# Layer 0 of a four-layer gated Flamingo stack: the first two expert routings ahead of other side jobs, two guessed experts' weights loaded before the first plan

## Chip, cores and metric

The kernel runs on one core of one Trainium2 chip. The metric is the device time of one execution in microseconds (us); lower is better. All data are float32 unless said otherwise.

## What is computed

The input x has 16 sequences of 128 tokens with 256 features; ctx has the same shape. Four layers follow each other, each a gated attention and a gated feed-forward part:

```
for i in 0..3:
    x = x + tanh(g_xattn[i]) * attention_i(layernorm(x), ctx)
    x = x + tanh(g_ffn[i])   * ffn_i(layernorm(x))
```

Attentions 0 to 2 have 16 heads of 16 features (attention 1 takes its softmax over the queries, attention 2 has a key mask), attention 3 has 8 heads of 64. The feed-forward parts of layers 0, 2 and 3 are mixtures of 8 experts with the top 2 per token; that of layer 1 is a dense layer with a routed low-rank addition. Layer 0's mixture, the one that matters here:

```
gate = softmax(x @ w_gate.T)                      # 8 experts
topk_scores, topk_idx = top_k(gate, 2)
h = gelu(x @ W1[e] + b1[e]); y = h @ W2[e] + b2[e]   # 256 -> 1024 -> 256
out = sum over the two chosen experts of score * y
```

## The kernel before, in words

**Tiles.** x stays in SBUF as 16 tiles of 128 tokens. Work goes in four blocks of four tiles. An attention is a loop over 16 items (one tile each): `scores(n)`, `values(n-1)`, `output(n-2)`, in `attend` (from L1411). `output` adds the result to x and `ready` takes the tile's layer-norm statistics (`mean_var`, L248, bn_stats and bn_aggr).

**Side jobs.** Everything else in the attention phase is a Python generator, a *job*, cut into stages by `yield`. `yield 1` asks for the next stage on DVE, `yield Act(1)` on ACT, `yield Pe(1)` on PE. For every block there are jobs that prepare the next block (layer norm, queries, keys; `prepare`, L1160), and when a block's last output is out, a *behind* job: in layers 0, 2 and 3 the routing `Moe.front` (L457). At the start of each block of items the loop waits until the preparing jobs are done.

**The planner.** While the kernel is being built, `Clock` (L1342) keeps a modelled time for PE, ACT, DVE and POOL, and `attend` places a job's next stage when the model says that its inputs are there and its engine's queue is short (`poll`, `whole`, `idle`, `Tick`). PE, ACT and DVE then execute in exactly this order. The orders of SP's and POOL's queues are chosen by the framework from modelled readiness, not by hand. Times of the model are not times of the chip.

**Routing and plan.** `Moe.front` normalises a block, computes router logits, picks the top two (`first_max` twice), gets each row's place by a rank matmul and running offsets, and POOL scatters each tile's rows twice into a DRAM table `xg` (8 indirect DMAs per block, L552). `xg` was filled with zeros before (`clear`, 15 DMAs of 1170 KB). After block 1 and after block 3 of layer 0 a *plan* (`Moe.plan`, L621) turns the counts into slots: a slot is 128 rows of one expert. The first plan holds only full slots, and 9 of them are certain for two blocks, whatever the routing; the second plan holds the other 30. A plan gives each slot its expert (row 0), its place (row 1) and *new* (row 2): 0 if the lane's weights are already those of this expert.

**Slots and lanes.** `Moe.slots` (L721) runs the slots of a plan. A lane is a set of weight buffers (w1 and w2 of 1024 KB, b1 4 KB, b2 128 KB). The first nine slots go over two lanes alternately: lane 0 takes the first five slots of the plan, lane 1 the last four, so the second slot executed is the sixth of the plan. Per slot SP reads plan values, loads the rows (`load`: xr, L782), and issues `first` (w1, b1, b2) and `second` (w2); a load whose *new* is 0 is skipped on the chip (`fetch`, L1575). PE transposes the rows (L815), computes the hidden layer (L1624), ACT takes Gelu (L1629), PE the second product (L852), DVE scales (L860), POOL scatters the result (L864). The slots are `attend`'s *filler*: its PE stages are placed only once all 16 items have had their scores; the PE stages of other jobs go ahead of it.

**Layer 1.** Its softmax sums run over the queries, per key. `Fast16.scores` sums four exponential tiles of 128x512 (L1264 to L1276): for two of them POOL first adds the two halves into a 128x256 tile (L1269), for the others DVE reduces all 512 columns (L1273).

Of the kernel before, what the change touches and what calls it, by code (L numbers as in the profile page):

```python
# [90 lines left out]
def kernel(ctx: ExitStack, tc: tile.TileContext, a: dict, out: bass.AP):  # L91
# [156 lines left out]
    def mean_var(mv, i, src):  # L248
        st = stat.tile([P, 6], F32, tag="bnst", name="bnst", bufs=4)
        nc.vector.bn_stats(st, src)  # L250
        nc.vector.bn_aggr(mv[:, i, :], st)

# [188 lines left out]
    class Moe:  # L441
# [4 lines left out]
        def __init__(self, layer, wg, turn, see=None):  # L446
            self.layer, self.wg, self.turn, self.see = layer, wg, turn, see
            self.off = rpool.tile([P, B + 1, NE], F32, tag="off", name="off", bufs=1)
            nc.gpsimd.tensor_copy(self.off[:, 0], region)
            self.carry = region  # L450
            self.done = None
            self.passed = 0
            self.scatters, self.returns, self.weighted = [], [], []

# [3 lines left out]
        def front(self, blk, plan=None, bias=None):  # L458


            own_set = run["fast"] and blk == NBLK - 1
            xns, xnT = yield from ln_block(blk, self.see, own_set, True)
            if bias is not None:
# [4 lines left out]
            next(soft)  # L468
            yield Act(1)
            next(soft)  # L470
# [10 lines left out]
            hot = self.kept([P, 2, BPB, NE], "hot")  # L481
            yield 1
            first_max(hot[:, 0], key, m, xns[:, :, D + 3])
            yield 1
            key2 = small("key2")
# [44 lines left out]
            )  # L530
            yield 3
            while self.passed < blk:
# [88 lines left out]
        def plan(self, turns, early=False, kind=""):  # L621
# [70 lines left out]
            nexts = [0] + ends[:-1]  # L692
            for lane in nexts:
                nc.vector.memset(plan[:, 2, lane:lane + 1], 1.0)

# [24 lines left out]
        def slots(self, n, plans, lanes, get, fetch1, fetch2, hidden, nf, far, depth):  # L720
# [151 lines left out]
            for s in range(near):  # L872
                load(s)
                first(s)
                if s < near2:
                    second(s)
# [6 lines left out]
            for s in range(n):  # L883
                while not planned(s + far + 1):
                    yield Pe(1)
                first(s + near)
                hT = yield from hidden(get, lane(s), xTs.pop(s), lambda *ps: when(s, *ps))
                if s == 0:
                    turn(1)
                turn(s + 2)  # L890
                hidden_of.append((s, hT))
                if len(hidden_of) > depth:
                    finish(*hidden_of.pop(0))
                weigh(s + 1)
                load(s + far)
                second(s + near2)
                yield Pe(0)
# [230 lines left out]
    class Fast16:  # L1128
# [86 lines left out]
        def scores(self, b, tick):  # L1215
# [45 lines left out]
            if layer == 1:  # L1261
# [4 lines left out]
                for j, e in enumerate(es):  # L1266
                    if j < 2:
                        half = pool.tile([P, 4, S // 2], F32, tag="half", name="half")
                        nc.gpsimd.tensor_tensor(  # L1269
                            half, e[:, :, 0:S // 2], e[:, :, S // 2:], ALU.add  # L1270
                        )
                        e = half
                    nc.vector.tensor_reduce(  # L1273
                        by_pair[:, j], e.rearrange("p (c e) s -> p c e s", e=2), AX.X, ALU.add
                    )
# [66 lines left out]
    class Clock:  # L1342


        def __init__(self):
            self.at = {e: 0.0 for e in (*IN_ORDER, mybir.EngineType.Pool)}
            self.done, self.read, self.rings = {}, {}, {}
            self.mode = None
            self.ends, self.moved = [], []

# [36 lines left out]
        def note(self, ins):  # L1387
# [5 lines left out]
            if "DMA" in type(ins).__name__ or ins.engine not in self.at:  # L1393
                end = max(start, self.at[PE]) + 3.0
                self.moved.append(end)
            else:
                start = max(start, self.at[ins.engine])
                end = start + self.cost(ins, outs[0], srcs)
                self.at[ins.engine] = end
                end += 0.2 if ins.engine == PE else 0.1  # L1400
                self.ends.append(end)
            for x in outs:
                self.done[x.tensor.name] = end
            for x in srcs:
                name = x.tensor.name
# [4 lines left out]

    def attend(parts, filler=None, open_end=False, hurry=True, share=2.5, eager=False):  # L1411

# [5 lines left out]

        clock = Clock()
        n = 0  # L1420
# [24 lines left out]
        def poll():  # L1445
            for job in jobs + filling:
                if job[2] is Pe:
                    continue
# [30 lines left out]
        class Tick:  # L1479
            left = 0.0  # L1480

            def __call__(self, full=True):
                if not full:
                    poll()
                    return
                end = now() + self.left
# [4 lines left out]

            def urgent(self):
                for job in jobs:
                    if job[3] and job[2] is Pe and max(job[1], bank()) <= now() + 0.1:
                        run_stage(job)
                        self.urgent()
                        return
# [24 lines left out]
        with tc.manual_schedule(engines=IN_ORDER):  # L1522
# [5 lines left out]
            for n in range(len(steps) + 2):  # L1528
# [22 lines left out]
                if n >= 2:  # L1551
                    att, b = steps[n - 2]
                    att.output(b, tick)
                    if b % BPB == BPB - 1:
                        _, _, behind, blk = blocks[(n - 2) // BPB]
                        job = begin(behind(blk), int, hurry)
                        waiting.append(job)
                        if len(waiting) <= 2:
                            jobs.append(job)
                    tick()  # L1560
# [6 lines left out]
    def gate_weights(name):  # L1567
# [5 lines left out]
        return wg  # L1573

    def fetch(out, weights, layout, e, new):  # L1575

        nc.sync.dma_start(
            out=out, in_=weights[bass.ds(e, 1)].rearrange(layout, p=P),
            cond=new, bounds_check="skip_entire_dma",
        )  # L1580

    def fetch_columns(out, name, e, new):
        n = out.shape[-1]
        nc.sync.dma_start(
            out=out, in_=a["cols"][:, bass.ds(e * n + _COLS[name][0], n)],
            cond=new, bounds_check="skip_entire_dma",
        )

    def fetch_row(out, rows, e, new):

        nc.sync.dma_start(
            out=out, in_=rows[bass.ds(e, 1), :].to_broadcast([P, D]),
            cond=new, bounds_check="skip_entire_dma",
        )

    def lane0(pool, n):
# [6 lines left out]
        } for _ in range(n)]  # L1603

    def slots0(moe, n, plans, lanes, get):
        nf = F0 // P

        def fetch1(w, e, new):
            fetch(w["w1"], a["l0_w1"], "e (k p) f -> p (e k) f", e, new)
            fetch_columns(w["b1"], "l0_b1", e, new)  # L1610
            fetch_row(w["b2"], a["l0_b2"], e, new)

        def fetch2(w, e, new):
            fetch(w["w2"], a["l0_w2"], "e (c p) d -> p (e c) d", e, new)

# [678 lines left out]
    def layers(fast):  # L2294
# [40 lines left out]
        with tc.tile_pool(name="context", bufs=1) as cpool, ExitStack() as for_mid:  # L2335
# [16 lines left out]
            with tc.tile_pool(name="att0", bufs=2) as pool:  # L2352
# [16 lines left out]
                def clear(blk):  # L2369
                    if blk == 1:  # L2370
# [9 lines left out]
                        for i in range(0, ROWS, n * P):  # L2380
# [268 lines left out]
```

## Time and profile before

| | |
|---|---|
| time, median of 3 runs | 1668.66 us (1667.05 to 1671.42) |
| profiled execution: its own time | 1609.76 us |
| profiled execution: span, first to last instruction | 1607.8 us |
| mean granted TensorE clock | 0.970 |
| busy share: PE, PE weight load, DVE, ACT, POOL | 93%, 73%, 54%, 40%, 24% |
| instructions | 34920 |
| DMA, mean over the span | 105 GB/s |
| layer 0's attention, first scores to last value matmuls | about 25 to 121.7 us |
| layer 0's first nine slots, hidden layers | 145.2 to about 220 us |

A line of the order of instructions reads: start (us from the span's start), duration, engine, source line, operation, output<-inputs, shape, count merged, and in brackets how long the engine was idle before it and what ended that. PE is TensorE's matmuls, PEld its weight loads, DVE VectorE, ACT ScalarE, POOL GpSimd, SPq the queue of SyncE, from which most DMAs are issued; an issue's duration is that of the issue, not of the transfer. A group's line ends in busy us and mean ns of one instruction, then the idle time ahead of them and what ended it.

### The profile page before, as it was taken

The page shows a single profiled execution, that of the slowest core. Times are in us where ns is not written, and L with a number is a line of the kernel's source. Part 1 is how long each engine was busy: PE and PEld are TensorE (multiplying, and loading weights), DVE is VectorE, ACT ScalarE, POOL GpSimd, SP SyncE. Part 2 cuts the span into 40 slices and gives each one's busy share as a digit, 9 for nine tenths or more (in the row PEclk, how much of TensorE's full clock was granted, in tenths as well). Part 3 has the DMA queues.
Part 4 walks back from the last instruction along what each step waited for, and adds up shares of the span by engine and source line. Part 5 has one row for each costly group of instructions (what it writes and reads, how often), then busy time and mean ns, then how long its engine had stood idle before and what let it go on. Part 6 is the DMA issues. An engine that isn't in the chain of part 4 may idle for free.

```text
span 1607.8 us, 34920 instructions
## 1 busy us (share of the span) xinstructions
PE 1493.5 (93%) x12752; PEld 1176.1 (73%) x12752; DVE 860.7 (54%) x2763; ACT 646.7 (40%) x1546; POOL 392.1 (24%) x517
## 2 busy tenths in 40 slices
PE   6994999999988999999999999999999999997992
PEld 4674889999655566665459999999965656677892
DVE  3785412223258776676345555555754437477664
ACT  5663333335546455553224333333453233224110
POOL 4234301112454322434000110111142002023531
PEclk9997999999999999999999999999999999999996
DMA  9606573534420000111064331611242000033956
GB/s 330 256 29 230 175 258 113 185 105 134 96 43 1 1 1 15 55 41 54 0 211 151 100 111 49 211 31 29 88 111 41 1 14 28 1 101 108 315 175 212
DMA packets 107768, 169.29 MB, mean 105 GB/s; under 512 B 17081, under 2 KB 77950, under 8 KB 107584
## 3 DMA queue, kind: packets, MB, share of 16 engines
q1 hardware_dynamic: 83744, 111.99, 22.1%
q0 software_dynamic: 20304, 49.66, 9.9%
q10 hardware_dynamic: 3536, 5.25, 1.0%
q8 instruction: 108, 1.77, 0.5%
q14 instruction: 76, 0.62, 0.1%
HBM read 268.42 MB, written 48.18 MB: 197 GB/s over the span
## 4 chain that ended last, share of the span: by engine, by line


## 5 line engine op out<-in xcount | busy, mean ns | idle before, releaser
L1801 PEld LDWEIGHTS ps_w<-xT,w 128*128 128x128 f32 x2304 | 264.3, 192 | 2.7 <-issue 0.4
L1801 PE MATMUL ps_w<-xT,w 128*128 128x128 f32 x2304 | 265.0, 275 | 0.2 <-issue 0.2
L864 POOL DMA_INDIRECT yd<-y,to x117 | 118.7, 1014 | 565.8 <-DVE c L827 296.8
L852 PE MATMUL ps_e<-w,hT 128*128 128x256 f32 x848 | 198.0, 380 | 2.5 <-DVE hT L1708 1.9
L852 PEld LDWEIGHTS ps_e<-w,hT 128*128 128x128 f32 x848 | 154.5, 190 | 21.6 <-DVE hT L1708 2.8
L1809 ACT ACTIVATE u<-ps_w,b 128x128 f32<-128x128 f32 x312 | 89.7, 368 | 175.8 <-PE ps_w L1801 170.7
L1624 PE MATMUL ps_h<-xT,w 128*128 128x128 f32 x1120 | 137.7, 283 | 12.4 <-DMA w<-in_l_w_dram 11.7
L1624 PEld LDWEIGHTS ps_h<-xT,w 128*128 128x128 f32 x1120 | 136.1, 200 | 15.6 <-issue 14.3
L1812 DVE SCALAR_TENSOR_TENSOR m<-ps_w,b,u 128x128 f32<-128x128 f32 x312 | 87.5, 344 | 109.1 <-PE ps_w L1801 93.8
L1629 ACT ACTIVATE hT<-ps_h,b 128x128 f32<-128x128 f32 x312 | 89.3, 373 | 119.4 <-issue 83.2
L552 POOL DMA_INDIRECT xg<-xn,xi x96 | 93.9, 978 | 108.3 <-issue 60.4
L1738 PE MATMUL ps_w<-xnT,sw 128*128 128x512 f32 x256 | 111.9, 593 | 0.0
L860 DVE SCALAR_TENSOR_TENSOR y<-ps_e,c,bias 128x256 f32<-128x256 f32 x78 | 37.6, 482 | 133.5 <-PE ps_e L852 129.7
L1110 POOL TENSOR_TENSOR sum_range<-sum_range,rs 128x256 f32<-128x256 f32 x48 | 35.4, 737 | 262.2 <-DVE rs L2218 136.3
L1738 PEld LDWEIGHTS ps_w<-xnT,sw 128*128 128x128 f32 x256 | 48.2, 190 | 56.8 <-issue 50.7
L817 DVE COPY xT<-ps_xr 128x256 f32<-128x256 f32 x117 | 48.4, 416 | 73.4 <-PE ps_xr L815 73.4
L1316 DVE RECIPROCAL rs<-ps_o 128x256 f32<-128x256 f32 x32 | 56.1, 1754 | 38.1 <-PE ps_o L1305 30.9
L1258 ACT ACTIVATE e<-ps_s 128x512 f32<-128x512 f32 x128 | 66.0, 602 | 21.8 <-PE ps_s L1243 21.8
L321 ACT ACTIVATE xn<-x,nmr,rstd 128x256 f32<-128x256 f32 x128 | 67.5, 595 | 16.3 <-DVE nmr L314 16.3
L844 ACT ACTIVATE bias<-b,c 128x256 f32<-128x256 f32 x78 | 40.3, 516 | 72.0 <-DMA b<-in_l_b_dram 28.1
L1305 PE MATMUL ps_o<-e,v 128*32 128x128 f32 x1536 | 54.3, 284 | 11.7 <-POOL sum_range L1110 4.7
L2197 ACT ACTIVATE e<-ps_s 128x512 f32<-128x512 f32 x64 | 33.4, 600 | 74.2 <-PE ps_s L2191 74.2
(273 smaller groups left out, 2578.7 us busy)
## 6 DMA issues: line engine op xcount, KB each, us to landing
w<-in_l_w_dram SPq DMA_DIRECT2D x156, 1024.0 KB
w<-in_l_w_dram SPq DMA_DIRECT2D x39, 512.0 KB
kT<-in_l_wgu_dram SPq DMA_DIRECT2D x39, 512.0 KB
xg<-zeros POOLq DMA_DIRECT2D x15, 1170.0 KB, 21.4
xr<-xg SPq DMA_DIRECT2D x78, 130.0 KB
b<-in_l_b_dram SPq DMA_DIRECT2D x78, 128.0 KB
kT<-in_l_w_dram SPq DMA_DIRECT2D x39, 256.0 KB
x<-yd POOLq DMA_DIRECT2D x48, 128.0 KB, 4.9
```

What stands on the lines that cost most here:

```text
L321: nc.scalar.activation(xns[:, i, 0:D], src, AF.Identity, bias=nmr[:, i:i + 1], scale=rstd[:, i:i + 1])
L552: self.unordered(nc.gpsimd.indirect_dma_start(out=xg[:, :], in_=xns[:, i, :], in_offset=None, out_offset=bass.IndirectOffsetOnAxis(ap=xi[: ...
L852: nc.tensor.matmul(po, lhsT=hT[:, f, :], rhs=lane(s)["w2"][:, f, :], start=(f == 0), stop=(f == nf - 1),)
L864: self.unordered(nc.gpsimd.indirect_dma_start(out=yd[:, :], in_=y, in_offset=None, out_offset=bass.IndirectOffsetOnAxis(ap=to[:, 0:1], axi ...
L1258: nc.scalar.activation(e, pss[j], AF.Exp)
L1316: nc.vector.reciprocal(rs, po[:, 1])
L1624: nc.tensor.matmul(ps[:, i, :], lhsT=w["w1"][:, k, f * P:(f + 1) * P], rhs=xT[:, k, :], start=(k == 0), stop=(k == KC - 1),)
L1629: nc.scalar.activation(hT[:, f, :], ps[:, i, :], AF.Gelu, bias=w["b1"][:, f:f + 1])
L1738: nc.tensor.matmul(ps, lhsT=wt[:, k, f * P:(f + 1) * P], rhs=xnT[:, k, :], start=(k == 0), stop=(k == KC - 1),)
L1801: nc.tensor.matmul(ps[:, f, :], lhsT=wt[:, k, s, f * P:(f + 1) * P], rhs=xT[:, k, :], start=(k == 0), stop=(k == KC - 1),)
L1809: nc.scalar.activation(u[:, f, :], pair[0][:, f, :], AF.Identity, bias=w["b1"][:, i:i + 1])
L1812: nc.vector.scalar_tensor_tensor(m1[:, f, :], pair[1][:, f, :], w["b3"][:, i:i + 1], u[:, f, :], ALU.add, ALU.mult,)
```

## The change

1. *Express routing.* In layer 0 the routings of blocks 0 and 1 are *express* (`express=2`): they are put at the head of the job list with priority 2, some of their yields fall away, their DVE and ACT stages are placed as long as the modelled queue is under 4 us, and their PE stages also at the short ticks inside an item.
2. *Guessed weights.* When block 2's preparation starts, all eight loads of lane 0 for expert 0 and of lane 1 for expert 3 are issued without condition, behind the last bn_aggr emitted by then. In the first plan, *new* for the first slot of each lane becomes "expert is not the guessed one" instead of 1. Within a slot b1 and b2 are now loaded ahead of w1. With two lanes, slot 0's w2 is asked for after slot 1's w1.
3. *Planner.* With `eager` (layer 0 only) the model gives DMAs of SP a shared transfer rate and POOL's DMAs an issue time; everywhere DMAs count as starting no earlier than the last plan.
4. *Layer 1.* The halving on POOL is gone; DVE reduces all four tiles over 512 columns.

```diff
-        nc.vector.bn_aggr(mv[:, i, :], st)
+        run["aggr"] = nc.vector.bn_aggr(mv[:, i, :], st).ins
...
+            express = run["fast"] and self.layer == 0 and blk < NBLK // 2
...
             next(soft)
-            yield Act(1)
+            if not express:
+                yield Act(1)
             next(soft)
...
-            yield 1
+            if not express:
+                yield 1
             first_max(hot[:, 0], key, m, xns[:, :, D + 3])
-            yield 1
+            if not express:
+                yield 1
...
-            yield 3
+            if not express:
+                yield 3
             while self.passed < blk:
...
-            for lane in nexts:
-                nc.vector.memset(plan[:, 2, lane:lane + 1], 1.0)
+            for lane, at0 in enumerate(nexts):
+                new = plan[:, 2, at0:at0 + 1]
+                if lane in self.guess:
+                    nc.vector.tensor_scalar(
+                        new, plan[:, 0, at0:at0 + 1], float(self.guess[lane]), None,
+                        ALU.not_equal,
+                    )
+                else:
+                    nc.vector.memset(new, 1.0)
...
-                if s < near2:
+                if s < near2 and near > 1:
                     second(s)
...
                 first(s + near)
+                if s == 0 and near == 1:
+                    second(0)
...
                 for j, e in enumerate(es):
-                    if j < 2:
-                        half = pool.tile([P, 4, S // 2], F32, tag="half", name="half")
-                        nc.gpsimd.tensor_tensor(
-                            half, e[:, :, 0:S // 2], e[:, :, S // 2:], ALU.add
-                        )
-                        e = half
                     nc.vector.tensor_reduce(
...
             if "DMA" in type(ins).__name__ or ins.engine not in self.at:
-                end = max(start, self.at[PE]) + 3.0
+                start = max(start, self.at[PE], self.plan)
+                if not self.loads:
+                    end = start + 3.0
+                elif ins.engine == mybir.EngineType.Pool:
+                    self.at[ins.engine] = max(start, self.at[ins.engine]) + 1.27
+                    end = self.at[ins.engine] + 2.5
+                else:
+                    size = self.free(outs[0]) * list(outs[0].ap)[0][1] * 4
+                    if outs[0].tensor.name in self.done and size > 2e5:
+                        size *= 0.3
+                    self.dma = max(self.dma, start) + size / 250e3
+                    end = self.dma + 2.0
...
             for job in jobs + filling:
-                if job[2] is Pe:
+                while job[3] == 2 and job in jobs and job[2] is not Pe:
+                    queue = max(now(), clock.at[DVE if job[2] is int else ACT])
+                    if job[1] > queue + 0.3 or queue > now() + 4.0 and job[1] > now():
+                        break
+                    run_stage(job)
+                if job[2] is Pe or job[3] == 2:
                     continue
...
                 if not full:
                     poll()
+                    self.urgent(2)
                     return
...
-                        job = begin(behind(blk), int, hurry)
+                        job = begin(behind(blk), int, 2 if blk < express else hurry)
                         waiting.append(job)
                         if len(waiting) <= 2:
-                            jobs.append(job)
+                            jobs.insert(0 if blk < express else len(jobs), job)
...
+    def first0(w, e, new):
+        fetch_columns(w["b1"], "l0_b1", e, new)
+        fetch_row(w["b2"], a["l0_b2"], e, new)
+        return fetch(w["w1"], a["l0_w1"], "e (k p) f -> p (e k) f", e, new)
...
+                    if blk == 2 and fast:
+                        moe.guess = {0: 0, 1: 3}
+                        for get_some in first0, second0:
+                            for lane, e in moe.guess.items():
+                                tc.add_manual_dep(
+                                    get_some(lanes[lane], e, None).ins, run["aggr"].name,
+                                    mybir.DependencyInfo(
+                                        mybir.DependencyClass.Sync,
+                                        mybir.DependencyReason.DATA,
+                                    ),
+                                    reason="behind the first loads",
+                                )
...
-                    attend([(att, clear, behind)], early(), eager=True)
+                    attend([(att, clear, behind)], early(), eager=True, express=2)
```

More of the change, by code (lines that the diff above doesn't have):

```diff
@@ L452, in __init__ @@
             self.passed = 0
+            self.guess = {}
             self.scatters, self.returns, self.weighted = [], [], []
@@ L692, in plan @@
             nexts = [0] + ends[:-1]
-            for lane in nexts:
-                nc.vector.memset(plan[:, 2, lane:lane + 1], 1.0)
+            for lane, at0 in enumerate(nexts):
[7 more added lines that the diff above has]
+                    nc.vector.memset(new, 1.0)
+            self.guess = {}
             nc.vector.tensor_copy(plan[:, 3], end[:, NE - 1:NE].to_broadcast([P, n]))
@@ L1342, with __init__ @@
     class Clock:
-        def __init__(self):
+        def __init__(self, loads):
+            self.loads = loads
             self.at = {e: 0.0 for e in (*IN_ORDER, mybir.EngineType.Pool)}
@@ L1348, in __init__ @@
             self.mode = None
+            self.dma = self.plan = 0.0
             self.ends, self.moved = [], []
@@ L1403, in note @@
                 self.done[x.tensor.name] = end
+                if x.tensor.name.startswith("plan_i"):
+                    self.plan = end
             for x in srcs:
@@ L1409, in when, with attend @@
             return max((self.done.get(t.tensor.name, 0.0) for t in tiles), default=0.0)
-    def attend(parts, filler=None, open_end=False, hurry=True, share=2.5, eager=False):
-        clock = Clock()
+    def attend(parts, filler=None, open_end=False, hurry=True, share=2.5, eager=False, express=0):
+        clock = Clock(eager)
         n = 0
@@ L1490, in __call__, with urgent @@
                 poll()
-            def urgent(self):
+            def urgent(self, least=1):
                 for job in jobs:
-                    if job[3] and job[2] is Pe and max(job[1], bank()) <= now() + 0.1:
+                    if job[3] >= least and job[2] is Pe and max(job[1], bank()) <= now() + 0.1:
                         run_stage(job)
-                        self.urgent()
+                        self.urgent(least)
                         return
@@ L1573, in gate_weights, with when_new @@
         return wg
+    def when_new(new):
+        return {} if new is None else {"cond": new, "bounds_check": "skip_entire_dma"}
     def fetch(out, weights, layout, e, new):
-        nc.sync.dma_start(
+        return nc.sync.dma_start(
             out=out, in_=weights[bass.ds(e, 1)].rearrange(layout, p=P),
-            cond=new, bounds_check="skip_entire_dma",
+            **when_new(new),
         )
@@ L1585, in fetch_columns @@
             out=out, in_=a["cols"][:, bass.ds(e * n + _COLS[name][0], n)],
-            cond=new, bounds_check="skip_entire_dma",
+            **when_new(new),
         )
@@ L1592, in fetch_row @@
             out=out, in_=rows[bass.ds(e, 1), :].to_broadcast([P, D]),
-            cond=new, bounds_check="skip_entire_dma",
+            **when_new(new),
         )
@@ L1603, in lane0, with second0 @@
         } for _ in range(n)]
+    def first0(w, e, new):
+        fetch_columns(w["b1"], "l0_b1", e, new)
+        fetch_row(w["b2"], a["l0_b2"], e, new)
+        return fetch(w["w1"], a["l0_w1"], "e (k p) f -> p (e k) f", e, new)
+    def second0(w, e, new):
+        return fetch(w["w2"], a["l0_w2"], "e (c p) d -> p (e c) d", e, new)
     def slots0(moe, n, plans, lanes, get):
         nf = F0 // P
[L1608 to L1614, printed above, removed]
+        fetch1, fetch2 = first0, second0
         def hidden(get, w, xT, when):
```

## The prediction

> **What bounds the kernel now.** I read first the busy times by stage, then the order of instructions where TensorE (PE) has a hole, then the SP queue, then the groups of layer 1. By stage (columns: length, then busy us of PE, PE weight load, DVE, ACT, POOL, granted PE clock, DMA share, GB/s):
>
> ```profile
> 100.00:110.00 10.00, 9.90 (x196) 8.12 (x197) 5.48 (x13) 6.60 (x15) 4.48 (x7) 1.00 0.13 43
> 110.00:120.00 10.00, 10.00 (x191) 8.12 (x193) 9.24 (x28) 5.19 (x12) 1.47 (x2) 1.00 0.01 3
> 120.00:130.00 10.00, 5.08 (x80) 3.70 (x72) 9.31 (x30) 3.13 (x6) 5.75 (x6) 1.00 0.19 68
> 130.00:140.00 10.00, 2.11 (x22) 1.44 (x21) 9.00 (x46) 2.19 (x5) 3.89 (x7) 0.69 0.46 138
> 140.00:150.00 10.00, 5.42 (x24) 5.08 (x25) 2.27 (x14) 2.76 (x6) 5.86 (x6) 0.50 0.99 309
> 150.00:160.00 10.00, 7.01 (x39) 6.80 (x38) 1.26 (x6) 4.82 (x15) 1.92 (x2) 0.67 1.05 383
> 160.00:170.00 10.00, 10.00 (x72) 9.59 (x72) 2.37 (x12) 3.17 (x9) 1.00 (x1) 0.94 0.24 62
> ```
>
> PE sets the pace nearly everywhere (93% of the span; 40 of 40 us in each stretch from 240 to 400). From 120 to 160 it works 19.6 us of 40: 20.4 us idle, behind DVE first (9.3 and 9.0 of 10), then behind the transfers (0.99 and 1.05). The order of instructions tells why:
>
> ```profile
> 121.86 0.16 DVE L631 SCALAR_TENSOR_TENSOR have<-off,region 128x8 f32<-128x8 f32 x1
> ...
> 131.69 0.96 POOL L552 DMA_INDIRECT xg<-xn,xi  x1 [0.30 <-issue]
> ...
> 134.60 0.19 DVE L698 CAST plan_i<-plan 128x36 int32<-128x36 f32 x1
> ...
> 136.78 0.37 SPq L782 DMA_DIRECT2D xr<-xg  x1
> ...
> 138.10 0.38 SPq L1577 DMA_DIRECT2D w<-in_l_w_dram  x1
> ...
> 145.24 6.49 PE L1624 MATMUL ps_h<-xT,w 128*128 128x128 f32 x32 [4.44 <-DMA w<-in_l_w_dram]
> 146.08 0.39 SPq L1577 DMA_DIRECT2D w<-in_l_w_dram  x1
> ...
> 155.16 3.75 PE L1624 MATMUL ps_h<-xT,w 128*128 128x128 f32 x16 [2.99 <-DMA w<-in_l_w_dram]
> ```
>
> Attention's last value matmuls end at 121.7. The first expert slot starts at 145.2, after the last row scatter of block 1 (132.65), the plan (134.8), the rows (xr) and a 7.1 us weight load. Slot 1 waits again. The gap also cools PE: slot 0's 32 matmuls take 6.49 us, those at 167.95 take 3.73; slot 1's two halves take 3.75 and 2.29 for 1.87 each. That excess is 2.8 + 1.9 + 0.4 = 5.1 us. **To be won: 20.4 + 5.1 = 25.5 us.**
>
> **Part 1, routing of blocks 0 and 1 first.** Block 1's last statistics end at 88.76, its positions (xi) at 121.95: 33 us. The same chain without yields: DVE about 40 small steps at 0.16 to 0.23 (7.5 us), four normalisations on ACT (2.1), Ln, Exp, copies (2.0), PE transposes, logits, ranks (3.0): 14.6 us. Some seven changes of engine wait behind attention's pieces (exponentials 2.06, reciprocals 1.76); at about 0.8 each that is 5.5. Sum 20: xi at 109. Eight scatters at 1.27 apart and a landing of 2.6 follow: rows complete at 122; the plan's 5.4 us of DVE run beside them. So the first xr load goes at about 122.3 instead of 136.78. It then took 3.4 us to the transposes (140.14); copy and hops another 1.3: slot 0 at 127 instead of 145.2.
>
> The work is moved, not added. What it is moved past: DVE is 32.6 of 40 us busy from 80 to 120. Block 1's tail and the plan (8.3 us summed from their rows) come in, block 0's tail (5.3) goes out ahead of 80: 35.6 of 40. It fits, with little room. If the room is not where it is needed, the net 3 us lie on attention's path, if it is, none: I take 1.5, its end at 123 instead of 121.7.
>
> **Part 2, weights of experts 0 and 3 ahead.** They wait for the last row statistics emitted before them (near 50 us); behind them on SP nothing stands until the first xr. Eight DMAs, 2 x (1024 + 1024 + 128 + 4 KB) = 4.5 MB, issued where SP has nothing from 19.4 to 134.6. They meet the zero fill of xg, which runs at about 390 GB/s to 67. The Trainium skill ("DMA: Bandwidth & Descriptors", Queues, rings and completion order) says each DMA engine takes turns among the queues that have work. By that rule the fill's last 6.5 MB share with the 4.5 and end near 78; by the trace's order (fill issued first) they end at 67 and the weights at 78. Block 0's scatters, now at 92.7, come at about 80 and must follow the fill: by the one they wait 0 to 1 us on POOL, by the other none. The range sums that queue behind them hold DVE's rs buffers; I charge 0.5.
>
> Is the guess right? The reference's gate on its inputs gives block 0 and 1 the counts 255, 280, 252, 209, 353, 270, 194, 235; full slots in order are 0,1,1,2,3,4,4,5,5. Lane 0 takes the first five, lane 1 the last four, so lane 1 begins with expert 4, not 3. The SP queue agrees: a column load that is skipped takes 0.08, one that goes 0.34 to 0.51,
>
> ```profile
> 153.22 0.51 SPq L1584 DMA_DIRECT2D b<-in_cols_dram  x1
> ...
> 169.92 0.08 SPq L1584 DMA_DIRECT2D b<-in_cols_dram  x1
> ```
>
> and over the nine slots goes, goes, goes, skipped, skipped, goes, goes, skipped, goes: just this list taken lane by lane. **So half the guess hits.** Slot 0 finds its weights; slot 1 loads 2.2 MB all the same. Its w1 was issued 9.3 us after the first xr; slot 0's skipped loads save 2 us of that (0.37 from one skipped load to the next, against 0.6 to 1.2), the new order within a slot (b1 and b2 ahead of w1) gives 1.2 back: 8.5 after, 130.8. Landing took 7.1 and 9.1 us behind 0.8 to 2.3 MB of other loads; with 0.7 MB of rows ahead, at 385 GB/s, I take 5 us (bounds 3 and 9): slot 1 at 135.8 instead of 155.2.
>
> What stays of the 25.5: about 3 us between attention's tail and slot 0, 3 between slots 0 and 1 (131 to 135.8, less some 2 us of block 2's matmuls that fit in), 1.5 of slower attention, 0.5 POOL, 1.5 cold clock. On the clock the rule and the row differ: "TensorE: Matmul & The Clock Gate" (Part 1) lets the clock drop to half after about 3.4 us idle and not before. Here it is 0.50 from 135 to 150, after stretches of mostly idle PE, and 0.91 at 200 to 220 with one gap of 2.5, after which 32 matmuls took 5.44 for 3.73. The rule would charge 0 for gaps of 3 and 2; the row charges 1.7 per gap; I take 1.5. Sum 9.5, **gain 16**.
>
> Who is late next: the second plan, done at 185.8, is first used about 217. Slots 2 to 8 move up to 200; the routings of blocks 2 and 3 no longer share DVE with the plan. Slack 14 even if they don't move: no new wait.
>
> **Part 3, layer 1 without the POOL halves** (455 to 580):
>
> ```profile
> L1273 DVE TENSOR_REDUCE sums<-e 128x4 f32<-128x512 f32 x32 | 20.3, 676 | 0.0
> L1273 DVE TENSOR_REDUCE sums<-half 128x4 f32<-128x256 f32 x32 | 13.0, 417 | 22.4 <-POOL half L1269 22.4
> ```
>
> 32 reductions grow by 0.26: +8.3 us DVE. DVE's 22.4 us of waits for POOL go. At 575.6 the four sums end at 578.66; started straight from the first exponentials (575.5) at 0.68 each they end near 578.3. That is 0.4 x 16 = 6 at most, where PE idles some 13 us in the stage, mostly on other chains. Lower bound -3 (DVE late for other work), upper +4; I take 1.5.
>
> **Part 4, the planner's new DMA times** outside layer 0: rows only due after the plan. It moves orders in layer 3; no row prices it; -2 to +2, taken 0.
>
> **Sum.** 16 + 1.5 = 17.5 us. The profiled execution was 1609.76 (span 1607.8 and 2 around it): it would be 1592.3. The median of the runs shown is 1668.66, 58.9 above, which no row of the trace explains; I take the gain across one to one: **1651**.
>
> **Rivals.**
> - *SP in the way.* At 134.56 SP issues three loads of later attention weights ahead of the first xr; they had waited for attention 0's last reads of their place (DVE at 130.99, POOL at 134.54). If they still stand ahead, the xr loads wait for attention's end, now perhaps 130: slot 0 at 135, slot 1 at 143.5; gain 9, with layer 1 10.5: 1658. For it: that order now. Against: the order is made from readiness, and rows will be ready first.
> - *Better.* Chain 16 us, layer 1 the full 4, one cold start less: 22 of the 25.5, and 4: gain 26, 1643.
> - *No change.* Routing comes forward but slots don't, because lane 1's reload, queued with slot 2's, holds PE as before: 1666.
> - *Slower: attention is starved.* Before items 8 and 12 the loop waits for the queries of the next block, and the express routings stand ahead of them on ACT, DVE and PE. If all of each routing's 14.6 us went on that path, 29.2 us would be added against 17.5 won: 1680. It decides once attention's last value matmul goes past about 140 (my 123 and the 17.5). Against it: DVE's room above, ACT 6.6 and 5.2 of 10.
>
> **Numbers.** Forecast as worked 0.55; better 0.12; SP 0.18; no change 0.08; slower 0.07. So faster by over 0.3% (5 us, about what a measurement here can tell from none) 0.85, within it 0.08, slower 0.07. Main case 1645 to 1657 by the bounds of chain, landing and layer 1; with the SP and better cases 1641 to 1663.
>
> **What would show it.** xi of block 1 near 109, first xr near 122, slot 0 near 127 with no weight wait, slot 1's column load going (not skipped) and its start near 136; PE idle in 120 to 160 about 8; the second plan no later than 186; layer 1 shorter by 0 to 4. I am wrong if attention ends past 126, if SP shows attention weights ahead of xr, if slot 1's load is skipped, or if the gain at slot 2 is lost by the end of layer 0.

## The result and the profile after

| | before | after |
|---|---|---|
| time, median of 4 runs each | 1668.82 us (1667.05 to 1671.42) | 1653.84 us (1650.62 to 1656.77) |
| ratio after/before, 95% interval | | 0.9903 (0.9878 to 0.9929) |
| profiled execution: its own time | 1609.76 us | 1650.62 us |
| span | 1607.8 us | 1648.9 us |
| mean granted TensorE clock | 0.970 | 0.960 |
| busy PE, DVE, ACT, POOL (us) | 1493.5, 860.7, 646.7, 392.1 | 1520.9, 863.6, 649.4, 368.4 |

The time is 15 us shorter, close to the 17.5 that were forecast. But the profile after is 41 us *longer* than the profile of before, so the two can't be subtracted. **The runs of this case fell on several chips, and these are not alike:** on some the kernel before takes 1664 to 1670 us, on one 1607. The first profile of before looks like the second kind, the timed runs are of the first. This decides how everything below is read. Each chip was used during one stretch of time only, so what is put down to the chip here could also belong to that time.

The changed kernel by stage, with the columns of the stages before:

```profile
120.00:130.00 10.00, 7.57 (x98) 4.76 (x96) 6.49 (x23) 2.44 (x5) 6.05 (x7) 1.00 0.19 68
130.00:140.00 10.00, 8.76 (x110) 5.99 (x112) 6.06 (x22) 4.00 (x10) 3.42 (x5) 0.66 0.12 43
140.00:150.00 10.00, 7.55 (x102) 6.05 (x91) 8.33 (x26) 5.20 (x9) 1.60 (x3) 1.00 0.38 103
150.00:160.00 10.00, 5.28 (x34) 5.04 (x33) 3.83 (x22) 8.37 (x16) 0.00 (x0) 0.77 0.58 204
```

From 120 to 160 PE is idle 10.8 us instead of 20.4. Only part of this is won: some of what now fills the hole is attention itself, which runs on to 141, and at a granted clock of 0.66 from 130 to 140. The DMA share at 140 to 160, 0.99 and 1.05 before, is now 0.38 and 0.58, so what holds PE is no longer the transfers. The order of instructions names it (the last scatter of block 1, 32 matmuls at the slow clock, the plan, the first rows, a skipped column load, attention's last value matmuls, a column load that goes, slots 0 and 1):

```profile
131.08 0.96 POOL L558 DMA_INDIRECT xg<-xn,xi  x1 [0.30 <-issue]
...
134.62 1.94 PE L1315 MATMUL ps_o<-e,v 128*32 128x128 f32 x32
...
137.63 0.18 DVE L712 CAST plan_i<-plan 128x36 int32<-128x36 f32 x1
...
138.80 0.36 SPq L796 DMA_DIRECT2D xr<-xg  x1
...
140.14 0.10 SPq L1618 DMA_DIRECT2D b<-in_cols_dram  x1
...
140.19 1.06 PE L1315 MATMUL ps_o<-e,ones 128*32 128x128 f32 x32
...
145.77 0.34 SPq L1618 DMA_DIRECT2D b<-in_cols_dram  x1
...
147.80 3.84 PE L1659 MATMUL ps_h<-xT,w 128*128 128x128 f32 x32 [0.85 <-DVE xT L831]
...
156.80 6.39 PE L1659 MATMUL ps_h<-xT,w 128*128 128x128 f32 x32 [4.72 <-DVE xT L831]
```

Half the guess hits as forecast: lane 0's loads are skipped (0.10 us), lane 1's go (0.34 us), and no attention weight stands on SP ahead of the first xr. Against the forecast, attention ends at 141.2, not 123, and slot 1 waits for its transposed rows (DVE), not for its weights. In layer 1 the reductions stand as one group, at 0.68 us each as costed:

```profile
L1283 DVE TENSOR_REDUCE sums<-e 128x4 f32<-128x512 f32 x64 | 39.4, 677 | 5.7 <-ACT e L1274 5.5
```

### The profile page after: what moved, and what is told of

Same layout as the page of the kernel before. It is cut to its first block, busy times and chain, and to the rows that moved or that the text cites. A ratio compares the mean times of both kernels' runs of the same rounds, so it can differ in the third digit from the quotient of the medians.

```text
span 1648.9 us, 34879 instructions
## 1 busy us (share of the span) xinstructions
PE 1520.9 (92%) x12752; PEld 1188.3 (72%) x12752; DVE 863.6 (52%) x2763; ACT 649.4 (39%) x1550; POOL 368.4 (22%) x485
## 4 chain that ended last, share of the span: by engine, by line
## 5 line engine op out<-in xcount | busy, mean ns | idle before, releaser
L1659 PE MATMUL ps_h<-xT,w 128*128 128x128 f32 x1120 | 136.7, 282 | 11.5 <-DVE xT L831 6.1
L874 DVE SCALAR_TENSOR_TENSOR y<-ps_e,c,bias 128x256 f32<-128x256 f32 x78 | 37.6, 482 | 135.8 <-PE ps_e L866 130.3
L1326 DVE RECIPROCAL rs<-ps_o 128x256 f32<-128x256 f32 x32 | 56.2, 1755 | 61.9 <-PE ps_o L1315 24.9
L831 DVE COPY xT<-ps_xr 128x256 f32<-128x256 f32 x117 | 48.6, 418 | 75.9 <-PE ps_xr L829 71.0
L1259 PE MATMUL ps_s<-qM,kT 32*128 32x256 f32 x768 | 61.5, 407 | 2.2 <-issue 1.2
## 6 DMA issues: line engine op xcount, KB each, us to landing
b<-in_l_b_dram SPq DMA_DIRECT2D x80, 128.0 KB
x<-yd POOLq DMA_DIRECT2D x48, 128.0 KB
```

Source lines behind the costliest of these rows:

```text
L1259: nc.tensor.matmul(pss[j][:, 2 * c:2 * c + 2, :], lhsT=self.kT[blk][part, c, tok], rhs=self.qM[blk][part, c, :, tok], start=True, stop=True,)
L1659: nc.tensor.matmul(ps[:, i, :], lhsT=w["w1"][:, k, f * P:(f + 1) * P], rhs=xT[:, k, :], start=(k == 0), stop=(k == KC - 1),)
```

## The experiments

Milestones of all profiles, in us from the start of the span; "layer 1" is the time from the end of layer 0's last hidden-layer matmul to the start of the first shared matmul (ps_w) of layer 1's feed-forward part. "Gaps" says whether the profile shows the short PE gaps of experiment 3. Each row is one profiled execution, and executions of one kernel differ by several us (before on one chip: 1601.77 to 1610.52), so differences of a few us between rows say little.

| kernel | gaps | xi of block 1 | attention 0 ends | slot 0 | slot 1 | layer 0 ends | layer 1 |
|---|---|---|---|---|---|---|---|
| before, first profile | no | 122 | 121.7 | 145 | 155 | 418.0 | 282.6 |
| before_again | yes | 128 | 127.8 | 152 | 162 | 429.3 | 293.5 |
| the change | yes | 121 | 141.2 | 148 | 157 | 428.1 | 284.5 |
| after_again | yes | 122 | 142.9 | 149 | 158 | 430.0 | 283.8 |
| right_guess | yes | 120 | 139.8 | 147 | 156 | 429.4 | 289.3 |
| halves_back | yes | 119 | 139.8 | 146 | 155 | 427.4 | 297.4 |
| express_only | yes | 121 | 139.5 | 155 | 167 | 432.0 | 294.9 |
| guess_only | yes | 127 | 126.8 | 152 | 160 | 423.6 | 299.7 |
| halves_only | yes | 128 | 128.0 | 151 | 161 | 431.1 | 283.3 |
| guess_halves | yes | 125 | 125.1 | 150 | 159 | 422.6 | 285.7 |
| guess_halves_2 | yes | 129 | 129.3 | 154 | 163 | 429.6 | 285.1 |
| halves_unread | no | 110 | 121.4 | 132 | 141 | 409.2 | 274.0 |
| express_late_scatter | no | 124 | 119.4 | 146 | 156 | 419.3 | 281.5 |
| scatter_twice | no | 127 | 127.6 | 149 | 160 | 424.7 | 281.6 |

**1. Where the 59 us between profile and median lie, and which layer holds the gain.** Four kernels on one chip. The first is the kernel before, unchanged:

> The kernel before, profiled once more, because the first profile (1609.76 us) lies 59 us under the median of its other executions. Theory A (that profile is the odd one): this profile is near 1668, and its extra time is spread over PE's own sequence, as short gaps between matmuls and matmuls that take longer. Theory B (the first profile shows the usual course, and what is outside the span differs): about 1610 again.

It took 1666.13 us (span 1664.3), in line with the median. For the same 12752 matmuls PE is busy 1525.1 us instead of 1493.5 and idle 139.2 instead of 114.3, at a clock of 0.954 instead of 0.970: the 56.5 us of span lie in slower matmuls (31.6) and in more idle time (24.9), all along the kernel.

The second is the whole change without its layer 1 part:

```diff
                 for j, e in enumerate(es):
+                    if j < 2:
+                        half = pool.tile([P, 4, S // 2], F32, tag="half", name="half")
+                        nc.gpsimd.tensor_tensor(
+                            half, e[:, :, 0:S // 2], e[:, :, S // 2:], ALU.add
+                        )
+                        e = half
```

> The change with only its layer 1 part undone (POOL adds the halves of two tiles again). Theory A (layer 0 pays): ratio to before about 0.991 to 0.993, as the whole change, 0 to 4 us slower than it. Theory B (layer 1 pays, since slot 0 of layer 0 starts at 147.8 us in the profile after, later than the 145.2 in the first profile before): ratio 0.996 or more.

1665.35 us against 1666.65, ratio 0.9993 (0.9978 to 1.0008). **Layer 0's parts and the planner together bring about 1 us, within the noise, not 16.** The third and fourth split them, both with the halves on POOL:

```diff
-            express = run["fast"] and self.layer == 0 and blk < NBLK // 2
+            express = False
...
-                    attend([(att, clear, behind)], early(), eager=True, express=2)
+                    attend([(att, clear, behind)], early(), eager=True, express=0)
```

> Weights ahead and the planner's new DMA times, but no express routing and no layer 1 part. Theory A (the express routing is what brings slots forward): within 4 us of before, ratio 0.998 to 1.002; slot 0 saves only its own weight load, some 3 to 5 us, where rows come late anyway. Theory B (the weight load was the wait that ended last): 8 us or more faster, ratio under 0.996.

```diff
-                    if blk == 2 and fast:
+                    if blk == 2 and False:
```

> Express routing and the planner's new DMA times, no weights ahead and no layer 1 part. Theory A (routing sets slot 0): 8 to 12 us faster than before, ratio 0.993 to 0.995, with slot 0 waiting some 5 us for its weights. Theory B (weights set slot 0): within 4 us of before.

guess_only: 1661.76 us, ratio 0.9974 (0.9960 to 0.9989), 4 to 5 us of gain. express_only: 1666.92 us, 0.9996 (0.9978 to 1.0013), none. In express_only block 1's positions come 7 us sooner than in before_again (121 for 128), but attention ends 12 us later (139.5 for 127.8) and slot 0 starts later too (155 for 152). With the guess, too, express costs time on this chip: halves_back, which has both, is 3.6 us slower than guess_only.

**2. Layer 1 alone, and the guess with and without express.** Four kernels on another chip (before there: 1669.94 us). The first is before without the halves on POOL, nothing else; the second is the change without express (`express = False` and `express=0`, as in guess_only); the third differs from the change in one number, shown here; the fourth is the change again.

```diff
-                        moe.guess = {0: 0, 1: 3}
+                        moe.guess = {0: 0, 1: 4}
```

> The kernel before with only layer 1's halving on POOL removed. Theory A, layer 1 holds nearly the whole gain of the change: 11 to 13 us below before, ratio 0.992 to 0.9935; layer 0 as before (first slot near 152, last hidden layer near 429), the value scaling of layer 1 ends near 581 instead of 589. Rival B, the gain needs both parts together (the planner's DMA times or the earlier slots): ratio above 0.997. My prediction's own size for this part: 1.5 us, ratio 0.999.

> The changed kernel without the express routing: weights of experts 0 and 3 ahead, planner, layer 1 without the halves. Theory A, parts add up and express brings nothing: 4.3 from the guess and 12 from layer 1, some 16 us below before, ratio 0.990 to 0.991, equal to the change or a few us better. Rival B, express only pays together with the weights (rows and weights both early): this kernel is slower than the change by 4 us or more.

> The changed kernel with lane 1 guessed as expert 4, which the routing really gives it, instead of 3. Theory A, slot 1's load is what holds TensorE between slots 0 and 1: slot 1 starts near 152 instead of 157 and 3 to 5 us stay to the end, ratio 0.987 to 0.989. Rival B, the gap only moves on to slot 2, which needs a new expert in lane 0: slot 1 early, slot 2 at 167 as before, time as the change within 1 us, ratio 0.990 to 0.992.

> The changed kernel once more, beside the other three on the same chip, so that their ratios can be set against its own: 0.988 to 0.993, the interval of the first comparison.

halves_only: 1654.44 us, ratio 0.9917 (0.9889 to 0.9945). That is as much as the whole change gains, from the one edit that the prediction priced at 1.5 us; rival B fails. after_again: 1658.54 us, 0.9929 (0.9903 to 0.9955). guess_halves: 1646.98 us, 0.9879 (0.9852 to 0.9906), 11.6 us below the change on the same chip; rival B, that express pays together with the weights, is contradicted here. right_guess: 1651.99 us, 0.9897 (0.9867 to 0.9927), within the intervals of the change, and slot 1 starts 9 us after slot 0 as in the change, although its loads are now skipped: **the load was not what held slot 1**; both theories of that run are wrong on this point. What held it stands on ACT, DVE and PE of the changed kernel:

```profile
149.92 1.14 ACT L1664 ACTIVATE hT<-ps_h,b 128x128 f32<-128x128 f32 x4
151.08 1.28 ACT L385 ACT_TABLE_LOAD   x1
...
152.61 1.28 ACT L237 ACT_TABLE_LOAD   x1
...
154.12 1.28 ACT L239 ACT_TABLE_LOAD   x1
...
155.64 1.28 ACT L1664 ACT_TABLE_LOAD   x1
...
155.66 0.16 DVE L242 SCALAR_TENSOR_TENSOR nt<-r,ve 128x4 f32<-128x4 f32 x1 [6.38 <-ACT r L239]
...
156.32 0.75 DVE L831 COPY xT<-ps_xr 128x256 f32<-128x256 f32 x2
```

Between the Gelu of slot 0 and that of slot 1, ACT serves block 2's softmax (Exp L385) and block 3's layer norm (Ln L237, Exp L239), and each of the three, and then Gelu, loads a table in 1.28 us. DVE waits 6.38 us for the result of L239, behind three of these loads (3.84 us), with slot 1's transposed rows (L831) queued behind, and PE waits 4.72 us for those. The kernel itself loads a table with both Ln and Exp (L294, at 146.37), but slot 0's Gelu loads its own at 148.63, before the first of the three. In before L294 stands at 131.07, and the same three activations run from 135.2 to 136.1 without a further load. No run moved these activations, so this is read from the trace alone. Profiles with express and guess together have 8 such loads from 120 to 240 us, those with only one of the two or neither have 4 or fewer. With both, slot 0 starts 6.6 us after attention's last value matmuls (before_again: 23.8), and the softmax that follows them is not done; in before it was when slot 0 began.

**3. How express delays attention, and whether it was POOL's load or DVE's wait in layer 1.** First what raised the question. The changed kernel while POOL issues block 1's scatters (one each 1.27 us):

```profile
124.15 0.43 PE L1315 MATMUL ps_o<-e,ones 128*32 128x128 f32 x5 [0.30 <-issue]
125.61 0.44 PE L1315 MATMUL ps_o<-e,ones 128*32 128x128 f32 x5 [0.30 <-issue]
126.35 1.12 PE L1337 MATMUL ps_y<-w_att,oT 128*128 128x256 f32 x4 [0.30 <-issue]
```

PE waits for nothing that the profile shows, yet works only some five matmuls in each 0.74 us. This is seen from 124 to 133 us, scatters at 122 to 132. In before_again block 1's scatters run from 129 to 139, behind attention's end at 127.8. So express may have pulled them onto attention's last items. Elsewhere the gaps go with scatters too: from 80 to 235 us before_again has such gaps (of 0.15 us or more) only at 94.9 to 99.9 (block 0's scatters run from 91.4 to 101.3) and at 190.7 to 195.0 (block 3's from 182.3 to 192.1). But not every scatter brings them: beside block 2's, which run from 170.6 to 180.4 in the change, matmuls pass without one. Three kernels on a third chip were to test it: the change with the POOL additions done but unread; express_only with block 1's scatters held back; and before with block 0's scatters issued twice.

```diff
                 for j, e in enumerate(es):
+                    if j < 2:
+                        half = pool.tile([P, 4, S // 2], F32, tag="half", name="half")
+                        nc.gpsimd.tensor_tensor(
+                            half, e[:, :, 0:S // 2], e[:, :, S // 2:], ALU.add
+                        )
                     nc.vector.tensor_reduce(
```

> The changed kernel, in which POOL still adds the halves of two exponential tiles per item in layer 1 (32 additions of 0.77 us), but nobody reads them: DVE reduces all four tiles in full. Theory A, what cost time before was DVE's wait for the halves: the ratio stays that of the change, 0.990 to 0.993. Rival B, what cost time was POOL's load itself, since the watch sums and residual additions queue behind the halves and TensorE waits for them (4.6 us of waits for POOL's sum_range in layer 1 of before): the gain goes, ratio 0.997 to 1.0, and those waits come back.

```diff
+            while express and blk == 1 and not run.get("late"):
+                yield Pe(1)
             xi = self.kept([P, 2, BPB], "xi", I32)
```

> The express-only kernel (no guessed weights, halves as before), in which the position cast of block 1 and with it its eight row scatters are held back in the order until attention 0's last value matmuls are placed; all other express steps stay where they are. Theory A, express stretches attention 0 because the scatters now fall on its last items and TensorE issues only some five matmuls per 0.74 us beside them: attention's last value matmul comes at 129 to 133 instead of 139.5, time 1660 to 1667. Rival B, the express stages themselves stand in the way of the next block's queries: it stays at 137 or later.

```diff
+            for i in range(BPB if self.layer == 0 and blk == 0 else 0):
+                for j in range(2):
+                    self.unordered(nc.gpsimd.indirect_dma_start(
+                        out=xg2[:, :], in_=xns[:, i, :], in_offset=None,
+                        out_offset=bass.IndirectOffsetOnAxis(ap=xi[:, j, i:i + 1], axis=0),
+                    ).ins, self.twice, "twice")
             release(xns)
```

> The kernel before with block 0's eight row scatters of layer 0 issued a second time, into a table of their own that nobody reads; TensorE's order is unchanged. Theory A, scatters slow TensorE while POOL issues them: short gaps of 0.3 us go on from 102 to 112 us, attention 0's last value matmul comes 3 to 5 us later than 128, time 2 to 5 us longer. Rival B, the gaps at 92 to 102 only coincide with the scatters: no further gaps, attention ends within 1.5 us of 128, time within 2 us of before.

On this chip before takes 1606.81 us (17 runs, 1601.77 to 1610.52). halves_unread: 1597.57 us, ratio 0.9949 (0.9931 to 0.9967). express_late_scatter: 1611.18 us, 1.0032 (1.0017 to 1.0047). scatter_twice: 1615.28 us, 1.0061 (1.0039 to 1.0084). None of the three shows gaps beside its scatters in attention 0. In halves_unread layer 0 is that of the change, and this is the same stretch, scatters of block 1 at 110.8 to 120.7:

```profile
117.40 1.06 PE L1320 MATMUL ps_o<-e,ones 128*32 128x128 f32 x32
118.38 1.13 PE L1342 MATMUL ps_y<-w_att,oT 128*128 128x256 f32 x4
119.44 1.08 PE L1320 MATMUL ps_o<-e,v 128*32 128x128 f32 x32
120.34 1.06 PE L1320 MATMUL ps_o<-e,ones 128*32 128x128 f32 x32
```

32 matmuls pass in one go, and attention ends at 121.4 with all of express' stages in its order, as early as in the first profile of before (121.7). So the stages themselves do not starve attention there; it is stretched where the gaps are (139.5 to 142.9 in five profiles with express, 125.1 to 129.3 in five without). Whether the scatters cause the gaps, or only go with them, was not settled: express_late_scatter and scatter_twice, meant for it, ran on the chip that has none, and the attention ends that their theories expected (129 to 133 or 137, and 3 to 5 us after 128) can't be held against 119.4 and 127.6 there. scatter_twice is slower for another reason. POOL's range sums queue behind the 16 scatters, DVE waits for a buffer (0.00 us busy from 100 to 110), and PE for DVE:

```profile
110.06 0.73 POOL L1118 TENSOR_TENSOR sum_range<-sum_range,rs 128x256 f32<-128x256 f32 x1
...
113.10 1.22 PE L1335 MATMUL ps_y<-w_att,oT 128*128 128x256 f32 x2 [6.45 <-DVE oT L1326]
```

Layer 1: with the additions on POOL still done but unread it lasts 274.0 us, where the three profiles of this kind that read them have 281.5 to 282.6. PE's wait for POOL's sum_range does not come back. So some 8 of the 11 us stay away although POOL's load is back: most of the cost was not that load but that DVE depended on POOL. (No kernel without the additions ran on this chip, so up to 3 us for the load can't be excluded; and the ratio, 0.995, lies between what the two theories expected.) The lines below are before_again's: the waits for POOL's halves in layer 1 (who waits, for whom, us in total, times, longest), then the first item.

```profile
DVE sums L1273 <- POOL half L1269: 21.5, 22, 4.7
```

```profile
464.97 1.90 POOL L359 TENSOR_TENSOR x<-x,rows 128x256 f32<-128x256 f32 x2
466.34 1.88 POOL L1269 TENSOR_TENSOR half<-e 128x256 f32<-128x256 f32 x2
...
467.58 0.42 DVE L1273 TENSOR_REDUCE sums<-half 128x4 f32<-128x256 f32 x1 [4.73 <-POOL half L1269]
...
470.75 1.51 PE L1305 MATMUL ps_o<-e,v 128*32 128x128 f32 x24 [4.63 <-POOL sum_range L1110]
```

The halves queue on POOL behind residual additions (L359), DVE stands 4.73 us, and all that DVE has to do next stands behind it. But the gain does not come wait by wait. The next table has the time from the end of layer 0 to the scaling of an item's values (`v`, L1278 in before_again, the first step that needs the sums), and before_again's waits for the halves up to it:

| item of layer 1 | before_again | halves_only | ahead by | waits so far |
|---|---|---|---|---|
| 1 | 40.9 | 36.5 | 4.4 | 5.0 |
| 6 | 71.0 | 70.1 | 0.9 | 11.5 |
| 10 | 100.7 | 99.0 | 1.7 | 17.4 |
| 12 | 124.2 | 118.3 | 5.9 | 18.6 |
| 16 | 160.0 | 152.5 | 7.5 | 21.5 |

After ten items 17.4 us have been waited and 1.7 won; against the waits that are gone stands DVE's own longer work (0.68 us a reduction for 0.42). From there to item 12 come 4.2 us, where before_again has 1.2 us of such waits. A second thing changed with this edit: the planner gives PE, DVE and ACT another order. Counting like matmuls in a row as one, PE's order in layer 1 differs between before_again and halves_only at some 24 places, while it is the same in halves_only, the change and halves_unread. One such place between items 10 and 12, first before_again, then halves_only:

```profile
537.10 1.88 PE L962 MATMUL ps_q<-xnT,w_att 128*128 128x512 f32 x4
...
546.33 1.98 PE L962 MATMUL ps_q<-xnT,w_att 128*128 128x512 f32 x4
```

```profile
539.80 3.70 PE L962 MATMUL ps_q<-xnT,w_att 128*128 128x512 f32 x8
```

No run kept the order of before and dropped the halves, so how much of the 11 us is DVE's wait and how much the new order stays open.

**4. The version without express once more.** The kernel guess_halves again, with an expectation for either kind of chip:

> The changed kernel without the express routing, once more. By now chips are seen to differ: on two of them TensorE shows 0.3 us gaps beside the row scatters and before takes 1667 to 1670 us; on one it shows none and before takes 1607, and there the whole change (with halves that nobody reads) ended layer 0 at 409 us and had ratio 0.995. If this run falls on a chip without gaps: theory A, express pays there and only there, since nothing stretches attention: without it the first slot starts at 138 to 145 and layer 0 ends at 411 to 415; rival B, express pays nowhere: layer 0 ends at 406 to 410. If it falls on a chip with gaps: ratio 0.985 to 0.991 again, below the change's 0.990 to 0.993.

It fell on a fourth chip, with gaps (before: 1664.02 us): 1653.55 us, ratio 0.9937 (0.9914 to 0.9960). The expected 0.985 to 0.991 was missed, and the two ratios of this one kernel, 0.9879 and 0.9937, have intervals that do not meet: from chip to chip a ratio moves by more than its interval. Set side by side on one chip, this kernel was 11.6 us faster than the change and 7.5 faster than halves_only; on this fourth chip neither of those ran, and the change's own ratios (0.9903, 0.9929) were not bettered. What the guess adds is therefore not settled. halves_only, a deletion of six lines, is as good as the change.

## Why the prediction was right or wrong, point by point

The time, 1653.84, lies 2.8 us from the forecast, and that is luck: layer 0 was priced at 16 and brought about 1, layer 1 was priced at 1.5 and brought 11. Two terms were wrong by similar amounts in opposite directions.

- **"16 us in layer 0".** On the chips with gaps halves_back measures 1 us. On the chip without, halves_unread ends layer 0 at 409.2 instead of the 418.0 of before's first profile: 9 us. That is one profile against one, 1594.1 against 1609.76 us in all, where the medians on that chip differ by 9.2 only; so it can be several us too much.
- **Block 1's xi at 109.** 110 on the chip without gaps, so the sum of the chain is right there. With gaps it is 119 to 122: attention is already slowed beside block 0's scatters, from 88 to 98 us, and every later item is late. Those scatters, forecast at about 80, start at 88.2 in the change and at 86.7 without gaps.
- **"1.5 us of slower attention, its end at 123".** 121.4 without gaps, 141.2 with them, where before_again has 127.8. Instead of 1.5 this costs 13.4 us, and in layer 0 it is the step that failed first. The cost is the gaps and, behind them, the clock: the 32 matmuls at 134.62 take 1.94 us, those at 140.19 take 1.06. The trace that the sum was made from has no such gap, so no row priced it. The rival "attention is starved" named the right point (past 140 the gain is spent) but not the mechanism: without gaps the express stages alone don't do it.
- **Slot 0 at 127.** Without gaps 132: the first xr goes at 123.0 (I had 122.3), but the transposes of its rows stand in PE's order behind attention's last outputs and block 2's logits, until 130.3. The sum had the rows as the only wait. With gaps, 148 for 152.
- **Slot 1 at 135.8 by the landing of its weights.** 141 without gaps; right_guess shows that the weights don't matter. The term that was left out is ACT's table loads: three of 1.28 us stand in DVE's wait, and PE stood 4.72 us. The Trainium skill ("ScalarE: Activation LUTs", What ACT_TABLE_LOAD costs) gives about 2.66 us for a change of set, drain included; here the load takes 1.28 and the next activation starts 0.01 to 0.02 later. By the page, as an estimate, the three alone would take 8.0 us, by the rows they take 3.84, and DVE's whole wait was 6.38.
- **Clock.** The row, not the rule. After slot 1's wait of 4.72 us its 32 matmuls take 6.39 for 3.73, which the rule that the prediction cites from "TensorE: Matmul & The Clock Gate" (Part 1: a drop after about 3.4 us idle) would give too. But a hole of 2.08 us is enough:

```profile
182.78 0.61 PE L499 MATMUL ps_rank<-both,tri 128*128 128x32 f32 x2 [2.08 <-DVE sm_s L388]
...
184.08 6.30 PE L866 MATMUL ps_e<-w,hT 128*128 128x256 f32 x16
```

  Those 16 take 3.62 elsewhere; the granted clock is 1.00 from 181 to 182 and 0.50 from 183 to 188. At 1.7 per gap I had the size for short gaps; these two cost 2.7 each.
- **Second plan, "slack 14, no new wait".** It comes at 202 instead of before_again's 197, and the tenth slot, the first that needs it, starts at 240 in both: no wait for it, but block 2's routing and block 3's layer norm no longer end ahead of the slots, which is where the table loads come from. Counted from 0, slots 4 and 5 start as late as in before_again (190 and 201 for 190 and 202), so the lead of slot 0 is gone by then.
- **"1.5 us in layer 1, upper +4".** Layer 1 lasts 293.5 to 299.7 us in the four profiles with gaps that have the halves, 283.3 to 289.3 in the six without: means 296.4 and 285.3, **11 us**. This is the other step that failed, a mis-sized term: I measured one item's chain and multiplied by 16; the 22.4 us of waits that the row showed were dismissed because PE idled little beside them, and that the order of layer 1 would change with the edit was not in the sum at all. The sums over layer 1 (length, then busy PE, PE weight load, DVE, ACT, POOL) of before_again and of halves_only say where the time was:

```profile
sum 294.00, PE 265.39 PEld 173.45 DVE 193.58 ACT 159.10 POOL 120.74; mean PE 22.12 PEld 14.45 DVE 16.13 ACT 13.26 POOL 10.06
```

```profile
sum 283.40, PE 260.88 PEld 172.47 DVE 198.43 ACT 158.26 POOL 97.85; mean PE 21.74 PEld 14.37 DVE 16.54 ACT 13.19 POOL 8.15
```

  DVE works 4.9 us more and the stage is 10.6 shorter: PE idles 28.6 and 22.5 us (6.1 less), and its matmuls take 4.5 us less for the same work. So the gain is in PE's idle time and in faster matmuls, 10.6 us where I allowed at most 4; as the table of experiment 3 shows, it can't be put down to DVE's 21.5 us of waits one by one.
- **Planner, 0.** From layer 1's shared part to the end the change takes 936.3 us and halves_only, with the old planner, 936.6: no difference that one profile each can show, as forecast.
- **"One to one across from the profile to the median".** It fails: the gain depends on the chip. Those 58.9 us that "no row explains" were the sign.

Rivals: SP was not in the way; "no change" is what happened in layer 0, but not by lane 1's reload. Open stay what sets the chips apart, whether scatters or something beside them cause the gaps, how layer 1's 11 us divide between wait and order, and what express is worth on a chip without gaps: the change itself was not run there, only with POOL's unread additions (0.995).

## What to carry to other kernels

A dependence between two engines can't be priced from the chain of one item: here sharing a reduction with POOL saved DVE 4.9 us of work and cost the layer 11 us, in waits and in the order that the planner makes around them, in a kernel whose PE looked 93% busy. Measure it by taking the dependence out, and then check whether the order of the other engines changed with it. When work is moved forward, look at which activation functions it will now stand between, and count a table load for every change that the trace shows. And when the profiled execution's time is 3.5% off the median, profile again before making sums from it; it may come from another chip.

## What the runs showed of the hardware that was not expected

- Chips of one type differ: before took 1666.65, 1669.94 and 1664.02 us on three and 1606.81 on a fourth. On the three, PE shows gaps of 0.3 us without a visible cause beside some of the indirect scatters, some five matmuls per 0.74 us; on the fourth 32 matmuls pass the same scatters in 1.06 us. (Chip and time of the runs can't be told apart.)
- A PE hole of 2.08 us was followed by matmuls at almost half speed (6.30 us for 3.62) and a granted clock of 0.50.
- In before one load of 1.28 us, asked for by the kernel (L294), serves Exp, Ln and Exp; when a Gelu came between that load and them, the same three activations got a load each.
